# First batch of a 1-head attention layer: weighted sum by seven products instead of eight, and the next batch's norm reading its input from two separately fetched blocks

## The chip, the cores and the metric

The kernel runs on one core of a Trainium2 chip. The metric is device time in microseconds (us), median over runs. The engines that matter are TensorE (matrix products; "PE" in the profile), VectorE ("DVE"), ScalarE ("ACT"), GpSimd ("POOL") and SyncE ("SP"), on whose queue every DMA of the part concerned is issued. TensorE writes into PSUM[...].

## The reference

Input: 4 images ("batches") of 512 channels and 32x32 = 1024 tokens, float32. Four layers follow each other, each adding to its input. The change lies in the third, one attention head as wide as all channels:

```python
xf = jnp.transpose(x, (0, 2, 3, 1)).reshape(b, h * w, c)       # tokens x channels
mu = jnp.mean(xf, axis=-1, keepdims=True)
var = jnp.var(xf, axis=-1, keepdims=True)
xn = (xf - mu) * jax.lax.rsqrt(var + EPS) * norm_w
qkv = jnp.einsum('bnc,dc->bnd', xn, w_qkv) + b_qkv
q, k, v = jnp.split(qkv, 3, axis=-1)
attn = jax.nn.softmax(jnp.einsum('bqc,bkc->bqk', q, k) * c ** (-0.5), axis=-1)
out = jnp.einsum('bqk,bkc->bqc', attn, v)
out = jnp.einsum('bnc,dc->bnd', out, w_proj) + b_proj
return x + transpose(out)
```

The layer before it (a linear attention) ends with an update of x; the one after it is a 4-head attention with a group norm. The first is an 8-head attention.

## The kernel before

**Tiles.** Channels lie on the 128 partitions in NC = 4 chunks, tokens in NTB = 2 blocks of TB = 512. An x of one batch is a tile of 2 MB; two of them fit into the on-chip memory, the others wait in DRAM ("homes"): `away(b)` stores x of batch b, `back(b)` loads it again. Other tiles are reused by name: a new tile of a name waits until all readers of the one before are done. Names that matter: `rds` (1 MB), `many` (1 MB), both used by the first layer's attention; `row` (3 buffers of one 512-wide row, for the norm's sums); `pt` (4) and `sum` (2), for the softmax's exponentials; PSUM has four banks `acc` and two pairs of banks `sc`, from which the norm's `lnsums`, the row sums and layer 2's products take theirs.

**Seven products.** Nearly every matrix product is done in 2x2 blocks by a scheme of seven block products and 15 sums (`seven_products`, L711-824). The sums of the inputs run on VectorE (`sum_inputs`), those of the weights on GpSimd (`sum_weights`, L695-698), and each result is put together from the products by copies on ScalarE (L746) and additions out of PSUM on VectorE, the joins (L737 and its neighbours).

**The 1-head layer, per batch** (loop at L1754): (1) queries, by seven products (records at L707), with the key weights folded in, so that the scores are taken against the normed x itself; (2) the values (`project_v`, L832), with the output weights folded in; (3) the scores (`keys_first`, L839), 8 tiles of 128 keys x 1024 queries made in pairs of blocks, each finished tile going to ScalarE for its exponential (`exp`, L1237) and from there into a running sum on VectorE (L1240); (4) the weighted sum of the values, together with the sums over the partitions (`row_sums`, L1256, two-bank tile `rowsum`), their reciprocals (`invert`, L678), and `add_block`: times the reciprocal (L1263), plus bias, plus x (L1265). Steps 3 and 4 are `one_head` (L1217-1378).

In step 4 batch 0 differs from the others. For batch 0, `one_head` gets a list `parts`; each of the 8 output tiles (4 channel chunks x 2 token blocks) is accumulated in one PSUM bank by 8 products of 128x128 by 128x512 (L1277), and ahead of each output tile one entry of `parts` is run. For batches 1 to 3 the sum is by seven products with shapes of their own (L1316): 56 products in place of 64, with 16 sums of value tiles (128x256) and 16 sums of exponentials (128x512) on VectorE, and ten joins.

**The norm of the next batch** (`layer_norm`, L1550-1593) has four parts for each token block: add (three additions over the channel chunks, L1557 and L1559), center (a product with ones gives the column sums, L1565; x less the mean, four at L1567; squares on ScalarE L1572, summed by three additions L1576), spread (a product with ones gives the variance, L1581; square root on ScalarE L1583, reciprocal L1584) and scale (four at L1589). It reads x of its batch from the 2 MB x tile.

**Order of the work.** TensorE's instructions keep the order in which the code issues them (a manual schedule covers all of it). Other work is threaded in by hand: `pieces` is a list of small pieces, `slot()` runs one, and `seven_products` calls it at its last `slots` pairs of calls and after every second product of its main part; `flush()` runs what is left. The other engines' instructions are ordered by the framework's scheduler; `soon()` gives some of them a higher priority.

While batch 0 runs, the list `pieces` also holds layer 2's last work, on batch 3: `linear_attention(B - 1)`, whose last two pieces are the updates of x (L1520). One more piece then stores x of batch 3 and loads x of batch 1. That is where batch 1's x gets its tile: the two tiles hold batch 0 and batch 3 until then. For this reason batch 1's norm is in `parts` (so in step 4), while those of batches 2 and 3 are in `pieces` from before step 2 of the batch ahead.

Ahead of the layer lies the end of the first layer's last attention: `sum_shared` (L1011) turns row sums into reciprocals, writes them to a DRAM tile `quotients` (L1030) and reads them back spread over all partitions into `rds` (L1033), where `normalise` multiplies them in (L1051). After this come loads of the 1-head layer's weights on the same SyncE queue: into the `v` tiles (L546) and `wo`.

Of the kernel before, what the change touches and what calls it, by code (L numbers as in the profile page):

```python
# [13 lines left out]
F32 = mybir.dt.float32  # L14
# [4 lines left out]
P = 128  # L19
# [455 lines left out]
def plain_path(ctx: ExitStack, tc: tile.TileContext, d: dict, out: bass.AP, count):  # L475
# [23 lines left out]
    def acc_tile():  # L499
        return ps_acc.tile([P, TB], F32, tag="acc", name="acc")  # L500
# [7 lines left out]
    def pt_tile(name):  # L508
        return work.tile([P, 2, TB], F32, tag="pt", bufs=4, name=name)
# [4 lines left out]
    def many_tile(name):  # L514
        return work.tile([P, NC, TB], F32, tag="many", name=name)
# [9 lines left out]
    def chunks_tile(tag, name, bufs=1):  # L525
        return work.tile([P, NC, TB], F32, tag=tag, bufs=bufs, name=name)


    def load_wqkv(src):
        t = wpool.tile([P, NC, 3 * C], F32, tag="wqkv", name="wqkv")  # L530
        nc.sync.dma_start(t, src.rearrange("(c p) o -> p c o", p=P))
        return t

    def load_wo(src):
        t = wpool.tile([P, NC, C], F32, tag="wo", name="wo")
        nc.sync.dma_start(t, src.rearrange("(c p) o -> p c o", p=P))
        return t
# [33 lines left out]
    def away(b):  # L571
        homes[b] = dram.tile([P, NC, S], F32, tag=f"home{b}", bufs=1, name=f"home{b}")
        nc.sync.dma_start(homes[b], xs.pop(b))

    def back(b):
        nc.sync.dma_start(x_tile(b), homes.pop(b))
# [89 lines left out]
    def both(*fs):  # L666
        return lambda: [f() for f in fs]
# [8 lines left out]
    def invert(rd, ps):  # L676

        nc.vector.reciprocal(rd, ps)  # L678
        n, m = next(unit), rd.shape[0]
        for i, t in enumerate((ps, rd)):  # L680
            closing[:] = [nc.vector.tensor_reduce(tops[:m, i, n : n + 1], t, AX.X, ALU.max).ins]
# [532 lines left out]
        while parts:  # L1214
            parts.pop(0)()

    def one_head(b, q, ws, acc, xn, sums, v, scale, bias, room, between, parts):  # L1217

# [31 lines left out]
        def row_sums():  # L1253
            rows = two_tile("rowsum")
            for t in range(NTB):
                nc.tensor.matmul(  # L1256
                    rows[:, t, :], lhsT=ones, rhs=acc[:, t, :], start=True, stop=True
                )
            return rows

        def add_block(m, tb, t, source, quotient):

            nc.vector.tensor_tensor(t, source, quotient, ALU.mult)  # L1263
            xv = x[:, m, bass.ts(tb, TB)]
            nc.vector.scalar_tensor_tensor(xv, t, bias[:, m : m + 1], xv, ALU.add, ALU.add)  # L1265

        flush()
        between()

        if parts:  # L1270
            rds = chunks_tile("q0", "rd")
            for k, (qb, m) in enumerate(itertools.product(range(NTB), range(NC))):
                if parts:
                    parts.pop(0)()
                out = acc_tile()
                for i, j in enumerate(order):
                    nc.tensor.matmul(  # L1277
                        out, lhsT=v[j // 2][:, j % 2, bass.ts(m, P)], rhs=pts[j][:, qb, :],
                        start=(i == 0), stop=(i == NT - 1),
                    )  # L1280
                if k == 0:
                    rows = row_sums()
                if m == 0:
                    invert(rds[:, qb, :], rows[:, qb, :])
                add_block(m, qb, rds[:, NTB + k % 2, :], out, rds[:, qb, :])
            return

# [257 lines left out]
        ]  # L1547


    def layer_norm(b, tb, tiles):  # L1550

        x = lambda c: xs[b][:, c, bass.ts(tb, TB)]
        t = {}

        def add():
            s = t["s"] = row_tile("s")
            nc.vector.tensor_tensor(s, x(0), x(1), ALU.add)  # L1557
            for c in range(2, NC):
                nc.vector.tensor_tensor(s, s, x(c), ALU.add)  # L1559

        def center():
            xn = tiles[tb]
            t["ps"] = two_tile("lnsums")
            mean = t["ps"][:, 0, :]
            nc.tensor.matmul(mean, lhsT=ones, rhs=t["s"], start=True, stop=True)  # L1565
            for c in range(NC):
                nc.vector.scalar_tensor_tensor(  # L1567
                    xn[:, c, :], mean, -1.0 / C, x(c), ALU.mult, ALU.add
                )
            for c in range(NC):  # L1570
                sq = row_tile("sq")
                nc.scalar.activation(sq, xn[:, c, :], AF.Square)  # L1572
                if c == 0:
                    t["sq"] = sq
                else:
                    nc.vector.tensor_tensor(t["sq"], t["sq"], sq, ALU.add)  # L1576

        def spread():
            xn = tiles[tb]
            var = t["ps"][:, 1, :]  # L1580
            nc.tensor.matmul(var, lhsT=ones, rhs=t["sq"], start=True, stop=True)  # L1581
            rstd = t["rstd"] = row_tile("rstd")
            nc.scalar.activation(rstd, var, AF.Sqrt, bias=eps, scale=1.0 / C)  # L1583
            nc.vector.reciprocal(rstd, rstd)  # L1584

        def scale():
            xn, rstd = tiles[tb], t["rstd"]
            for c in range(NC):
                nc.vector.scalar_tensor_tensor(  # L1589
                    xn[:, c, :], xn[:, c, :], col("nw2", c), rstd, ALU.mult, ALU.mult  # L1590
                )

        return [add, center, spread, scale]
# [64 lines left out]
    with tc.manual_schedule(engines={mybir.EngineType.PE}):  # L1658
# [63 lines left out]
        loadedv = load_bias(d["bv2"], d["wo2n"], vt[2:], brows[:, 1, :])  # L1722
        flush()
        wo2 = load_wo(d["wo2"])
        lin = linear_attention(B - 1, lambda i: pt_tile("l1"))

        norms[1][0]()
# [26 lines left out]
        for b in range(B):  # L1754
            q = q_tiles()
            vt = v_tiles()
            after = normed_tiles(b + 1)

            def sums():
                if b == 0:  # L1760
                    made.extend(sum_inputs(spare, normed(xn)))
                return made

            half = NC // 2
            seven_products(
                half,
                lambda i, j, o: gq[:, 2 * j : 2 * j + 2, bass.ts(i * half + o, P)],
                normed(xn),
                lambda i, o: uq[:, i * half + o : i * half + o + 1],
                lambda i, tb, o: q[tb][:, i * half + o, :],  # L1770
                sums,
                slots=2,
            )

            pair = lambda t, i: t[:, 2 * i : 2 * i + 2, :]
            halves = work.tile([P, 2, 2, TB], F32, tag="os", name="qs")
            third = work.tile([P, 2, TB], F32, tag="oi", name="qs")
            places = [halves[:, 0], halves[:, 1], third, pair(q[1], 0)]
            sum_weights(places, lambda i, j: pair(q[i], j))
            if b == 0:  # L1780
                pieces.append(lambda: (away(B - 1), back(1)))
            parts = []
            if b + 1 < B:
                (add0, *n0), (add1, *n1) = [layer_norm(b + 1, tb, after) for tb in range(NTB)]
            if b == 0:

                parts = [
                    both(add0, n0[0]), idle, both(*n0[1:], add1), idle, n1[0], idle,
                    both(*n1[1:]), lambda: sum_inputs(spare, normed(after)),
                ]  # L1790
            elif b + 1 < B:
                pieces.extend([
                    add0, n0[0], idle, n0[1], n0[2], add1, n1[0], idle, n1[1], n1[2],
                ])
            else:
                first = chunks_tile("ot", "gn")
                loaded3 = load_bias(
                    d["bv3"], d["wo3n"], [after[1][:, 2 * i : 2 * i + 2, :] for i in range(2)]
                )
                loads3 = []  # L1800
                pieces.extend([
                    *group_norm(0, 0, first),
                    lambda: loads3.append(weighted_bias("bo3", loaded3)),
                ])
            project_v(vt, hv, normed(xn), made, wpool.tile([P, NC, C], F32, tag="wo", name="ws"))
            one_head(
                b, q, places, work.tile([P, 2, TB], F32, tag="ou", name="acc"), xn, made, vt,
                float(C) ** -0.5, bo2,
                after if b == B - 1 else [w2[:, NC : 2 * NC, :], w2[:, 2 * NC :, :]],
                lambda: b + 1 < B or loads3.insert(0, load_wqkv(d["wqkv3"])), parts,  # L1810
            )
            if 0 < b < B - 1:
                sum_inputs(spare, normed(after))
            away(b)
            back((b + 2) % B)
            if b + 1 < B:
                xn = after
# [103 lines left out]
```

## Time and profile before

| | |
|---|---|
| median of 3 runs | 2450.09 us (2449.71 to 2451.28) |
| the profiled execution | 2450.76 us, its span 2449.0 us |
| ScalarE busy, share of the span | 704.6 us, 29% |
| GpSimd busy, share of the span | 251.1 us, 10% |
| batch 0's scores, TensorE | 1043.28 to 1093.66 us |
| batch 0's weighted sum, with batch 1's norm | 1093.66 to 1153.74 us |
| batch 1's weighted sum | 1254.42 to 1304.35 us |

The shares are from the page's first part, the stages from the chain of waits. The chain is followed back from the last instruction of the run, at each step to what released it or to the instruction before it on its engine; a piece of it reads: start in us, length in us, engine, what it writes, line, and how many records. One product of 128x128 by 128x512 in float32 makes two records. A row of a group reads: line, engine, operation, out<-in with shapes, count; then busy time and the mean ns of one record; then the idle time just ahead of them on their engine, with what ended it. Records on TensorE are pipelined and overlap, so their mean ns is longer than the time from one to the next. In the timeline a line reads: start, length, engine, line and operation, and in brackets the idle time ahead with its releaser. In the busy time by stretches each engine has its busy us and number of instructions, then the granted clock of TensorE (PEclk, 1.00 is full), the DMA engines' busy share and GB/s.

### The profile page before, as it was taken

The page shows a single profiled execution, that of the slowest core. Times are in us where ns is not written, and L with a number is a line of the kernel's source. Part 1 is how long each engine was busy: PE and PEld are TensorE (multiplying, and loading weights), DVE is VectorE, ACT ScalarE, POOL GpSimd, SP SyncE. Part 2 cuts the span into 40 slices and gives each one's busy share as a digit, 9 for nine tenths or more (in the row PEclk, how much of TensorE's full clock was granted, in tenths as well). Part 3 has the DMA queues.
Part 4 walks back from the last instruction along what each step waited for, and adds up shares of the span by engine and source line. Part 5 has one row for each costly group of instructions (what it writes and reads, how often), then busy time and mean ns, then how long its engine had stood idle before and what let it go on. Part 6 is the DMA issues. An engine that isn't in the chain of part 4 may idle for free.

```text
span 2449.0 us, 24662 instructions
## 1 busy us (share of the span) xinstructions
PE 2433.3 (99%) x10098; PEld 1225.7 (50%) x10098; DVE 1506.1 (61%) x1798; ACT 704.6 (29%) x864; POOL 251.1 (10%) x240
## 2 busy tenths in 40 slices
PE   9999999999999999999999999999999999999999
PEld 4544544453455344644645446445556456555653
DVE  3677577757775788656595774763554554445344
ACT  1454144415531653221211201112321430332132
POOL 4001100110010001101103021021010001002000
PEclk9999999999999999999999999999999999999999
DMA  5000020002000301011001010110010001001001
GB/s 185 7 12 18 5 78 10 18 5 79 19 9 13 130 23 48 5 69 39 31 1 69 5 74 13 52 69 18 35 69 1 18 35 52 1 35 35 1 22 45
DMA packets 28959, 88.64 MB, mean 36 GB/s; under 512 B 2508, under 2 KB 10188, under 8 KB 25895
## 3 DMA queue, kind: packets, MB, share of 16 engines
q1 hardware_dynamic: 28838, 87.00, 9.9%
q8 instruction: 81, 1.33, 0.2%
q14 instruction: 40, 0.32, 0.0%
HBM read 60.59 MB, written 25.35 MB: 35 GB/s over the span
## 4 chain that ended last, share of the span: by engine, by line
PE 99%; DVE 1%; ACT 0%; issue 0%; DMA 0%; SPq 0%; DVEq 0%
PE acc L707 20%; PE acc L832 12%; PE acc L967 9%; PE acc L982 9%; PE sc L936 9%; PE sc L931 9%; PE acc L839 8%; PE acc L1084 7%; PE acc L1316 6%; PE acc L1277 2%; PE feat L641 1%; PE acc L1018 1%; PE acc L641 1%; PE upd L1520 1%; PE acc L1454 1%; PE xt L1425 1%
## 5 line engine op out<-in xcount | busy, mean ns | idle before, releaser
L941 ACT ACTIVATE pt<-sc 128x1024 f32<-128x1024 f32 x384 | 379.2, 1022 | 541.2 <-PE sc L936 304.0
L950 DVE TENSOR_TENSOR sum<-sum,pt 128x1024 f32<-128x1024 f32 x256 | 314.6, 1229 | 159.0 <-ACT pt L941 146.5
L967 PE MATMUL acc<-pt,v 64*64 64x512 f32 x2048 | 247.6, 591 | 0.0
L931 PE MATMUL sc<-q,k 64*64 64x512 f32 x2048 | 245.0, 591 | 1.1 <-ACT pt L941 1.1
L982 PE MATMUL acc<-pt,v 128*128 128x512 f32 x512 | 240.8, 594 | 0.0
L936 PE MATMUL sc<-q,k 128*128 128x512 f32 x512 | 239.9, 594 | 0.0
L707 PE MATMUL acc<-t,ws 128*128 128x512 f32 x384 | 173.9, 594 | 0.0
L695 POOL TENSOR_TENSOR ws<-wqkv 128x256 f32<-128x256 f32 (+1 forms) x40 | 39.7, 992 | 1307.1 <-PE acc L1018 523.2
L947 DVE TENSOR_TENSOR sum<-pt 128x1024 f32<-128x1024 f32 x64 | 78.0, 1219 | 137.4 <-ACT pt L941 137.4
L982 PEld LDWEIGHTS acc<-pt,v 128*128 128x128 f32 x512 | 96.8, 190 | 125.1 <-issue 121.4
L936 PEld LDWEIGHTS sc<-q,k 128*128 128x128 f32 x512 | 97.1, 191 | 115.9 <-issue 92.7
L967 PEld LDWEIGHTS acc<-pt,v 64*64 64x64 f32 x2048 | 78.3, 133 | 142.5 <-issue 140.3
L931 PEld LDWEIGHTS sc<-q,k 64*64 64x64 f32 x2048 | 77.3, 133 | 140.9 <-issue 131.9
L707 PEld LDWEIGHTS acc<-t,ws 128*128 128x128 f32 x384 | 72.6, 190 | 86.5 <-issue 85.0
L746 ACT COPY v<-acc 128x512 f32<-128x512 f32 x24 | 14.0, 585 | 308.6 <-PE acc L832 308.6
L678 DVE RECIPROCAL rd<-acc 128x512 f32<-128x512 f32 (+1 forms) x24 | 80.5, 3353 | 29.1 <-PE acc L1018 29.1
L832 PE MATMUL acc<-ws,t 128*128 128x256 f32 x384 | 87.3, 380 | 0.0
L839 PE MATMUL acc<-qs,w 128*128 128x512 f32 x192 | 86.6, 593 | 0.0
L839 PE MATMUL acc<-q,ln 128*128 128x512 f32 x192 | 85.8, 593 | 0.0
L1084 PE MATMUL acc<-ot,wo 128*128 128x256 f32 x336 | 80.7, 383 | 2.7 <-ACT ou L1103 2.7
L737 DVE TENSOR_TENSOR v<-acc,v 128x512 f32<-128x512 f32 x72 | 49.5, 689 | 51.5 <-PE acc L832 51.2
L746 ACT COPY q<-acc 128x512 f32<-128x512 f32 x40 | 23.4, 585 | 197.1 <-PE acc L707 197.1
(326 smaller groups left out, 3476.0 us busy)
## 6 DMA issues: line engine op xcount, KB each, us to landing
home<-x SPq DMA_DIRECT2D x8, 2048.0 KB
x<-home SPq DMA_DIRECT2D x8, 2048.0 KB
out<-x SPq DMA_DIRECT2D x32, 256.0 KB
rds<-quotients SPq DMA_DIRECT2D x30, 256.0 KB
rds<-quotients SPq DMA_DIRECT2D x7, 1024.0 KB
x<-in_x SPq DMA_DIRECT2D x3, 2048.0 KB
wo<-in_wo SPq DMA_DIRECT2D x3, 1024.0 KB
w<-in_w SPq DMA_DIRECT2D x1, 3072.0 KB
```

Of the source, the lines that this page charges most:

```text
L678: nc.vector.reciprocal(rd, ps)
L707: nc.tensor.matmul(ps, lhsT=w[:, m, :], rhs=x[:, m, :], start=start, stop=stop, skip_group_check=True)
L832: nc.tensor.matmul(ps[:, bass.ts(r, C // 2)], lhsT=x[:, m, bass.ts(2 * o + r, P)], rhs=w[:, m, :], start=(start and r == 0), stop=stop, sk ...
L839: nc.tensor.matmul(ps, lhsT=x[:, m, bass.ts(o, P)], rhs=w[:, m, :], start=start, stop=stop, skip_group_check=True,)
L931: nc.tensor.matmul(ps[half(h), s, :], lhsT=key(g, i)[half(s), half(h)], rhs=q[qb][half(s), g, :], start=True, stop=True,)
L936: nc.tensor.matmul(ps[:, s, :], lhsT=key(g, 2 * i + s), rhs=q[qb][:, g, :], start=True, stop=True)
L941: exps.append(nc.scalar.activation(pt, ps, AF.Exp, scale=scale).ins)
L950: adds.append(nc.vector.tensor_tensor(acc, acc, pt, ALU.add).ins)
L967: nc.tensor.matmul(outs[qb, g][r][half(s), :], lhsT=v[i // 2][half(r), i % 2, g * P + s * hd : g * P + (s + 1) * hd], rhs=pt[half(r), s, : ...
L982: nc.tensor.matmul(outs[qb, g][0], lhsT=v[j // 2][:, j % 2, bass.ts(g, P)], rhs=pt[:, s, :], start=(j == 0), stop=(j == NT - 1),)
L1084: nc.tensor.matmul(ps[i][:, bass.ts(o, n)], lhsT=w[:, m, bass.ts(o, P)], rhs=t[:, m, :], start=(start and m + o == 0), stop=(stop and m == ...
L1316: nc.tensor.matmul(ps[i, o], lhsT=w[m][:, bass.ts(o, P)], rhs=t[m], start=(start and m == 0), stop=(stop and m == 3), skip_group_check=True,)
```

## The change

`one_head` loses the argument `parts` and the branch for batch 0, so all four batches take their weighted sum by seven products. The pieces of batch 1's norm now go into `pieces` ahead of step 2, as they do for the later batches. At that time x of batch 1 has no x tile yet, so `layer_norm` gets an argument `copies`: two 1 MB tiles, one for each token block, fetched from the same DRAM home. Block 0 is fetched into a tile of name `rds` before layer 2's pieces are put on the list; block 1 into a tile of name `many`, in the piece that also stores batch 3 and loads batch 1. The full x of batch 1 is still loaded as before, for the result's addition. Batch 1's sums of inputs, which were the last entry of `parts`, are now issued after `one_head`, as for batches 1 and 2.

```diff
-    def one_head(b, q, ws, acc, xn, sums, v, scale, bias, room, between, parts):
+    def one_head(b, q, ws, acc, xn, sums, v, scale, bias, room, between):
...
         flush()
         between()
-
-        if parts:
-            rds = chunks_tile("q0", "rd")
-            for k, (qb, m) in enumerate(itertools.product(range(NTB), range(NC))):
-                if parts:
-                    parts.pop(0)()
-                out = acc_tile()
-                for i, j in enumerate(order):
-                    nc.tensor.matmul(
-                        out, lhsT=v[j // 2][:, j % 2, bass.ts(m, P)], rhs=pts[j][:, qb, :],
-                        start=(i == 0), stop=(i == NT - 1),
-                    )
-                if k == 0:
-                    rows = row_sums()
-                if m == 0:
-                    invert(rds[:, qb, :], rows[:, qb, :])
-                add_block(m, qb, rds[:, NTB + k % 2, :], out, rds[:, qb, :])
-            return
...
-    def layer_norm(b, tb, tiles):
+    def layer_norm(b, tb, tiles, copies=None):
-        x = lambda c: xs[b][:, c, bass.ts(tb, TB)]
+        x = lambda c: copies[tb][:, c, :] if copies else xs[b][:, c, bass.ts(tb, TB)]
...
         wo2 = load_wo(d["wo2"])
+
+        copies = []
+
+        def copy_next(t):
+            nc.sync.dma_start(t, homes[1][:, :, bass.ts(len(copies), TB)])
+            copies.append(t)
+
+        copy_next(work.tile([P, NC, TB], F32, tag="rds", name="x1"))
         lin = linear_attention(B - 1, lambda i: pt_tile("l1"))
...
             if b == 0:
-                pieces.append(lambda: (away(B - 1), back(1)))
-            parts = []
+                pieces.append(lambda: (copy_next(many_tile("x1")), away(B - 1), back(1)))
             if b + 1 < B:
-                (add0, *n0), (add1, *n1) = [layer_norm(b + 1, tb, after) for tb in range(NTB)]
-            if b == 0:
-
-                parts = [
-                    both(add0, n0[0]), idle, both(*n0[1:], add1), idle, n1[0], idle,
-                    both(*n1[1:]), lambda: sum_inputs(spare, normed(after)),
+                (add0, *n0), (add1, *n1) = [
+                    layer_norm(b + 1, tb, after, None if b else copies) for tb in range(NTB)
                 ]
-            elif b + 1 < B:
                 pieces.extend([
                     add0, n0[0], idle, n0[1], n0[2], add1, n1[0], idle, n1[1], n1[2],
                 ])
...
-            if 0 < b < B - 1:
+            if b < B - 1:
                 sum_inputs(spare, normed(after))
```

More of the change, by code (lines that the diff above doesn't have):

```diff
@@ L1809, in plain_path @@
                 after if b == B - 1 else [w2[:, NC : 2 * NC, :], w2[:, 2 * NC :, :]],
-                lambda: b + 1 < B or loads3.insert(0, load_wqkv(d["wqkv3"])), parts,
+                lambda: b + 1 < B or loads3.insert(0, load_wqkv(d["wqkv3"])),
             )
-            if 0 < b < B - 1:
+            if b < B - 1:
                 sum_inputs(spare, normed(after))
```

## The prediction

> **What bounds the kernel now.** I read, in this order: busy time and the chain that ended last on the page, the groups by line and form around the change, the busy time of each engine in four stretches, VectorE's timeline of the next batch, and SyncE's timeline.
>
> ```profile
> PE 2433.3 (99%) x10098; PEld 1225.7 (50%) x10098; DVE 1506.1 (61%) x1798; ACT 704.6 (29%) x864; POOL 251.1 (10%) x240
> ...
> PE 99%; DVE 1%; ACT 0%; issue 0%; DMA 0%; SPq 0%; DVEq 0%
> ```
>
> TensorE is busy throughout and the chain runs along it: a product removed is time removed, unless a wait comes in.
>
> ```profile
> L1277 PE MATMUL acc<-pt,v 128*128 128x512 f32 x96 | 42.5, 593 | 0.0
> ...
> L1277 PE MATMUL acc<-pts,v 128*128 128x512 f32 x32 | 15.0, 593 | 0.0
> ```
>
> Batch 0's weighted sum is 128 records. The 593 ns overlap: the chain gives
>
> ```profile
> 1125.41 13.73 PE acc L1277 x32
> ...
> 1269.87 34.47 PE acc L1316 x80
> ```
>
> so a record takes 13.73/32 = 0.429 us of TensorE, a 128x512 product (two records) 0.858. Batch 1 computes the same sum by seven products, at the same pace (34.47/80 = 0.431).
>
> ```profile
> core 0: us, PE busy (x) PEld busy (x) DVE busy (x) ACT busy (x) POOL busy (x), PEclk, DMA share, GB/s
> 1062.00:1093.40 31.40, 31.40 (x76) 13.82 (x73) 21.28 (x29) 8.25 (x8) 0.00 (x0) 1.00 0.34 134
> 1093.40:1153.60 60.20, 60.20 (x142) 26.68 (x141) 48.20 (x54) 9.16 (x13) 2.35 (x2) 1.00 0.00 0
> 1204.40:1254.30 49.90, 49.90 (x117) 22.21 (x118) 34.23 (x50) 15.70 (x21) 0.00 (x0) 1.00 0.00 0
> 1254.30:1304.20 49.90, 49.90 (x118) 21.98 (x117) 41.39 (x56) 2.63 (x4) 5.13 (x5) 1.00 0.00 0
> ```
>
> Rows one and two are batch 0's scores (from where layer 1's last update leaves them) and weighted sum; three and four are batch 1's. Read the VectorE column: 21.28+48.20 = 69.5 of 91.6 us in batch 0. VectorE has slack here, but not much.
>
> ```profile
> 1269.91 3.36 DVE L678 RECIPROCAL ln<-rowsum 128x512 f32<-128x512 f32 x1 [3.37 <-PE rowsum L1256]
> ...
> 1274.92 3.35 DVE L678 RECIPROCAL ln<-rowsum 128x512 f32<-128x512 f32 x1
> ...
> 1279.31 0.68 DVE L1263 TENSOR_TENSOR ln<-acc,ln 128x512 f32<-128x512 f32 x1
> ```
>
> In batch 1 VectorE is ahead: it waits 3.37 us for the row sums. Its L1263 then frees a PSUM tile that TensorE's product at 1280.05 takes at once: no margin there if VectorE comes late.
>
> **What the Trainium skill says.** "Perfetto Trace Analysis", Identifying the Most-Contended Engine: matmul busy share does not tell how near the roofline a kernel is. The trace agrees: 99% says nothing of the spare product that seven products save. "VectorE: DVE Perf Modes", The TRN2 errata: an fp32 tensor_tensor of 512 columns takes 691 ns; the rows here have 680 to 693, and successive starts lie 0.60 apart. "TensorE: Matmul & The Clock Gate", HAM oscillation: idle gaps of TensorE over about 3.4 us can halve its clock; before has no such gap after its start (PEclk 1.00), so no run shows it. "DMA: Bandwidth & Descriptors", Bandwidth: 1 MB in 6.15 us; the trace's 2 MB store takes 6.4 us from issue to the next one, which gives 3.2 for 1 MB.
>
> **The change, part by part.**
>
> Removed: 64 products become 56. 8 x 0.858 = 6.87 us of TensorE. The four norm products (3.43) and two row sums (1.72) stay.
>
> Added on VectorE: seven products need 16 sums of 128x256 (spacing 0.34: 5.5 us), 16 of 128x512 (0.60: 9.6) and 10 joins (about 0.65: 6.5), 21.6 in all. Batch 0's scores and sum then hold 69.5+21.6 = 91.1 us of VectorE, less 1.8 for the first block's sums, which the built order has before 1062; TensorE's time shrinks to 91.6-6.87 = 84.7. VectorE becomes the bound. By total alone: 89.3 of work, and about 7 us before 1073 in which it still waits for the first score products (6.1 us of idle ahead of batch 0's L737 now), make 96: 5 us more than 91.6.
>
> Moved: both norms of batch 1 go from the weighted sum into batch 0's scores. Layer 1's pieces hold the slots up to 1062, so first norm, second norm and the score joins crowd into 31 us. By the built order TensorE's queue has: centre product (block 0) before the last joins of the first score half, spread product 8 products later, centre product (block 1) 12 later, spread product 4 later, then the weighted sum. TensorE runs in order, so each waits with everything behind it. I laid VectorE's instructions out in the built order, each as soon as VectorE is free and what it waits for is done, with durations from before (0.60 a 512 operation, 1.13 a 1024, 3.29 a reciprocal, 0.68 a scale, 0.34 a 256):
>
> 1. Centre product at 1072.8. VectorE first finishes an exp sum (to 1074.8), then 4 centres, 3 square sums, 4 score joins, another exp sum: 11x0.60+1.13 = 7.7, +0.2 latency: 1082.7. TensorE arrives at 1072.8+9x0.858 = 1080.5. Wait 2.3.
> 2. From 1082.6: exp sum 1.13, two adds of block 1's sum 1.2, two small sums 0.7, a join 0.6, reciprocal 3.3, five joins 3.0, four scales 2.7, exp sum 1.1, last add 0.7: 14.4, 1097.0, +0.3 for products not ready. TensorE arrives at 1082.8+13x0.858 = 1094.0. Wait 3.4.
> 3. Centre result at 1098.4; 4 centres, 2 joins, 3 square sums, an exp sum: 9x0.60+1.13 = 6.5, 1105.1. TensorE arrives at 1097.3+5x0.858 = 1101.6. Wait 3.5.
> 4. From 1105.0: exp sum 1.1, the norm's reciprocal and scales 6.0, and the weighted sum's sums (14x0.34, 13x0.60: 12.6) end at 1124.5. TensorE needs the first of them at 1105.1+17x0.858+1.72 = 1121.4 (made at 1118, no wait). But the row sums' first reciprocal starts at 1124.5, not at 1121.6: the join behind it ends 1129.1 where TensorE wants its PSUM tile at 1128.3 (wait 0.9), and L1263, after the second reciprocal, ends 1134.6 against 1132.6 (wait 2.1).
>
> Sum of waits 2.3+3.4+3.5+0.9+2.1 = 12.2; with spacings rounded up 12.7; I take 12.4. The same laying-out on before gives batch 1's product at 1280.0 (trace 1280.05) and no wait in batch 0 (trace: none). ScalarE's exps and squares are ready before VectorE asks; an extra table load (1.28) lies in its idle time.
>
> Fetches: two 1 MB loads on SyncE's queue.
>
> ```profile
> 904.10 0.53 SPq L1030 DMA_DIRECT2D quotients<-rd  x1
> ...
> 905.86 1.24 SPq L1033 DMA_DIRECT2D rds<-quotients  x2
> ...
> 916.06 3.82 SPq L546 DMA_DIRECT2D v<-in_wqkv  x2
> ```
>
> In the built order block 1's load stands ahead of the first of these. It waits for the product that reads `many`, done at 900.7, so it transfers 3.2 us (6.15 by the page) from about 901 and may hold the quotients back 0 to 2.5 us. Behind them waits VectorE's L1051 at 910.95; but VectorE idles 3.89 us at 933.31, before TensorE's next need: 0 (at most 1 if that cover fails). Block 0's load waits for L1051's reads and goes out near 912, ahead of the v loads at 916.06: 0. Both blocks land by 920 and are read after 1030. The store of batch 3 and load of batch 1 stay, now needed only at the end of batch 1.
>
> What follows: batch 1's sums of inputs (four 1.22) go after the sum as in the later batches, which show no wait for them; the store of batch 0 and load of batch 2 keep their distance to batch 1's start (18 us until first read). 0.
>
> Total -6.87+12.4 = +5.5 on the profiled execution, 2450.76 (span 2449.0 and 1.8 around it): 2456.3. The median shown is 0.67 below that run: 2450.09+5.5 = 2455.6.
>
> **Rivals.**
>
> A, hidden: VectorE keeps up and the whole 6.87 is gained, 2443.2. For: batches 1 and 2 do these products without waits. Against: their first norm lies in the v projection, where VectorE has room; here both norms share the scores. This needs 12.4 us less VectorE work on TensorE's path.
>
> B, half: the waits at the norm products hold, but VectorE catches up in the weighted sum (or spacings are tighter): the last two waits, 3.0, go: 2452.6, within the noise.
>
> C, more: waits of 3.4 and 3.5 us let TensorE's clock fall for a window each (half of 3.4 us lost, an estimate from the clock gate page), or the fetch delays the quotients: +1.7 to +3.4, 2457.3 to 2459.0. For: the gaps are as long as the window. Against: it must fall on a gap exactly.
>
> That the change doesn't do what it says: the built order has 56 products there, so no.
>
> **How the numbers follow.** VectorE-bound as laid out 0.64, A 0.06, B 0.15, C 0.15. A measurement of this kernel tells 0.2% (4.9 us) from no change: the line lies at 2455.0. The first case spreads over 2454.5 to 2457 and is beyond the line nine times in ten (0.58), with C 0.73 slower; its rest and B, 0.21 same; A, 0.06 faster. Range 2452.6 (B) to 2459.0 (C); it leaves out A and little else.
>
> **What would show it.** After: 112 records of weighted sum in batch 0; TensorE idle about 2, 3.5 and 3.5 us ahead of the three later norm products, released by VectorE's square sum, add and square sum; about 3 us in the weighted sum; VectorE busy without a break from 1073 to 1140; the rowsum reciprocal with no idle before it; L1051 at 911 nearly unmoved. Wrong if TensorE's chain has no such waits (A), if PEclk dips or L1051 waits some us longer (C), or if VectorE idles before the rowsum reciprocal (B).

## The result, and the profile after

The changed kernel takes 2457.3 us (median of 8 runs, 2456.22 to 2460.36) beside 2450.02 us before (8 runs, 2449.71 to 2451.28): ratio 1.0029, 95% interval 1.0020 to 1.0038. It is 7.3 us slower. The eight products are gone, and the time is not.

The profiled execution took 2460.36 us (span 2458.6), which is the longest of the eight, so its own surplus (9.6 us) is larger than the median's. The page's first part and its chain:

```profile
PE 2430.8 (99%) x10082; PEld 1218.5 (50%) x10082; DVE 1527.9 (62%) x1840; ACT 708.5 (29%) x868; POOL 253.3 (10%) x240
...
PE 96%; DVE 2%; issue 1%; DMA 0%; ACT 0%; SPq 0%; DVEq 0%
```

TensorE has 16 records fewer, VectorE 42 instructions and 21.8 us more. The chain, which lay on TensorE at 99%, now crosses over to VectorE for 2%. Where it does so is seen in TensorE's timeline; these are all of its waits from the scores to the end of the weighted sum (in brackets: idle time and releaser):

```profile
1083.14 1.78 PE L1565 MATMUL lnsums<-sq,ones 128*128 128x512 f32 x2 [2.08 <-DVE sq L1560]
1099.44 1.13 PE L1549 MATMUL lnsums<-s,ones 128*128 128x512 f32 x2 [3.18 <-DVE s L1543]
1108.82 1.13 PE L1565 MATMUL lnsums<-sq,ones 128*128 128x512 f32 x2 [3.12 <-DVE sq L1560]
1132.58 3.70 PE L1297 MATMUL acc<-w 128*128 128x512 f32 x8 [0.32 <-DVE ln L1307]
1138.17 3.70 PE L1297 MATMUL acc<-ts,ln 128*128 128x512 f32 x8 [1.89 <-DVE ln L1262]
```

Five waits, 10.59 us, all released by VectorE: first block's spread product, second block's centre and spread products, and two products of the weighted sum that need a PSUM tile. (These lines have numbers 16 to 19 smaller than in the kernel before: L1565 is the spread product, L1549 the centre, L1297 the weighted sum.) The busy time by stretches shows what VectorE had to do, and something else:

```profile
1062.00:1162.50 100.50, 89.91 (x201) 38.29 (x200) 88.42 (x121) 20.86 (x24) 6.26 (x6) 0.97 0.11 42
1083.48:1086.89 3.41, 3.41 (x5) 1.33 (x4) 2.62 (x5) 1.92 (x2) 0.00 (x0) 0.50 0.00 0
1100.55:1103.96 3.41, 3.41 (x6) 1.35 (x5) 1.93 (x4) 1.86 (x3) 0.00 (x0) 0.50 0.00 0
```

In the first row VectorE (third pair) is busy 88.42 us; before, it was 69.5 in the same work. In the other two the granted clock of TensorE (last number but two) is 0.50, for 3.41 us right behind the first wait and again right behind the second, where before had 1.00 throughout. Half of 3.41, 1.7 us, is lost in each of these two dips.

The balance of this execution, from the start of batch 0's scores (1043.56; before 1043.28) to the next batch's queries (1162.47; before 1153.74): 118.91 us for 110.46, so 8.45 longer. -6.87 for the products, +10.59 of waits, +3.4 for the two dips, and the remaining 1.3 for five restarts, about 0.27 each: without a wait the next record starts some 0.17 us before the one ahead of it has ended, and the two records behind a wait are followed by the next 0.96 us after their start (1108.82 to 1109.78) in place of 0.86. Outside the stage the two executions differ by 1.14: 0.28 ahead of it and 0.86 at the very end, behind the last product. The 0.28 is itself the sum of two things: the stretch with the fetch is 1.27 longer (see below), and up to there this execution was 0.99 ahead, 0.98 of it from the first 56 us, long before anything that the change touches.

### The profile page after: what moved, and what is told of

It reads as the page before. It is cut to its first block, busy times and chain, and to the rows that moved or that the text cites. A ratio compares the mean times of both kernels' runs of the same rounds, so it can differ in the third digit from the quotient of the medians.

```text
span 2458.6 us, 24682 instructions
## 1 busy us (share of the span) xinstructions
PE 2430.8 (99%) x10082; PEld 1218.5 (50%) x10082; DVE 1527.9 (62%) x1840; ACT 708.5 (29%) x868; POOL 253.3 (10%) x240
## 3 DMA queue, kind: packets, MB, share of 16 engines
q8 instruction: 81, 1.33, 0.2%
## 4 chain that ended last, share of the span: by engine, by line
PE 96%; DVE 2%; issue 1%; DMA 0%; ACT 0%; SPq 0%; DVEq 0%
PE acc L707 20%; PE acc L832 11%; PE acc L982 9%; PE sc L936 9%; PE acc L967 9%; PE sc L931 9%; PE acc L839 8%; PE acc L1084 7%; PE acc L1297 7%; PE feat L641 1%; PE acc L1018 1%; PE acc L641 1%; PE upd L1501 1%; PE acc L1435 1%; PE xt L1406 1%; PE kv L641 1%
```

## The experiments

Each was timed in five rounds beside the kernel before, on one chip for each group of four. "Laid out" in the expectations is the working of the prediction, repeated on the changed build: VectorE's instructions in their order, each as soon as VectorE and its inputs are ready.

**1. Filling the waits.** The question is whether the waits themselves or their effect on the clock account for all that exceeds the prediction's sum.

```diff
+        def fill(ps, n):
+            for _ in range(n):
+                nc.tensor.matmul(ps, lhsT=ones, rhs=bv1, start=True, stop=True)
...
+            if copies and tb:
+                fill(t["ps"][:, 1, :], 3)
             nc.tensor.matmul(mean, lhsT=ones, rhs=t["s"], start=True, stop=True)
...
+            if copies:
+                fill(var, 3 if tb else 2)
             nc.tensor.matmul(var, lhsT=ones, rhs=t["sq"], start=True, stop=True)
```

> The changed kernel with idle TensorE time before the three late norm products filled: 2, 3 and 3 spare products of 128x512 (0.86 us each) on constant data into the norm's own free PSUM half, ahead of the first spread, the second centre and the second spread product. Theory 1 (VectorE-bound waits of 2 to 3.5 us, and on top a lower TensorE clock after such gaps): fillers disappear in the waits, the granted clock stays at 1.00 from 1062 to 1142, and the time is 2450.0 + 3.2 (the laid-out waits less 6.87, the build shifting a few of VectorE's instructions in the weighted sum by 2.1 us in our favour) + about 1.3 for the fetch = 2453 to 2455. Theory 2 (the clock dips are chance and cost nothing in the median; what exceeds my sum is something else): 2457.3 - 2.1 = 2455.2 or more, with dips as before. If the waits are not waits for VectorE at all, the fillers add 8 x 0.86 = 6.9: 2464.

Measured: 2453.96 us against 2450.8, ratio 1.0014 (1.0008 to 1.0021): 3.2 us over before, where the changed kernel is 7.3 over, although TensorE does 6.9 us of work that nobody needs. TensorE's timeline and the busy time by stretches:

```profile
1081.61 1.12 PE L1573 MATMUL lnsums<-sq,ones 128*128 128x512 f32 x2 [0.36 <-DVE sq L1566]
1096.22 1.12 PE L1555 MATMUL lnsums<-s,ones 128*128 128x512 f32 x2 [0.60 <-DVE s L1547]
1104.05 1.13 PE L1573 MATMUL lnsums<-sq,ones 128*128 128x512 f32 x2 [0.69 <-DVE sq L1566]
...
```

```profile
1081.60:1085.00 3.40, 3.39 (x8) 1.63 (x9) 3.40 (x6) 1.97 (x2) 0.00 (x0) 1.00 0.00 0
...
1096.20:1099.60 3.40, 3.38 (x8) 1.63 (x9) 3.32 (x5) 1.45 (x3) 0.00 (x0) 1.00 0.00 0
1099.60:1103.00 3.40, 3.40 (x9) 1.25 (x7) 3.40 (x6) 3.25 (x5) 0.00 (x0) 1.00 0.00 0
```

The fillers vanish in the waits, which still end on the same VectorE operations, and the clock stays at 1.00 (last column but two). Of the 4.1 us between this kernel's surplus (3.2) and the changed kernel's (7.3), 1.8 are a shift of the build in its favour: fillers and waits together are 8.8 us in its trace (6.87+1.97), where the changed kernel waits 10.6. Some 2.3 remain for the clock and for what differs outside the stage, an estimate from one trace of each. That the dips come with the idle time and go with it is in the records.

**2. The norm moved, the plain products kept.**

```diff
+        if b == 0:
+            rds = chunks_tile("q0", "rd")
+            for k, (qb, m) in enumerate(itertools.product(range(NTB), range(NC))):
...
```

The loop is that of the kernel before, without `parts`.

> The changed kernel, but batch 0's weighted sum again by 64 plain products without the seven products' sums on VectorE; only the norm has moved and its x is fetched. Theory 1 (the crowd of norms and joins in the scores makes the waits): waits of 2.3 and 7.5 us before the two spread products, none in the weighted sum, no product saved: 2450.0 + 9.8 + 1.3 for the fetch + 1.7 to 3.4 for the clock = 2461 to 2465. Rival (the norm is free where it is now, the extra sums of the seven products are the cost): 2450 to 2452.

Measured: 2462.39 us, ratio 1.0048 (1.0034 to 1.0062): 11.6 us slower than before, as theory 1 has it. TensorE's timeline has two waits and no other:

```profile
1081.66 1.13 PE L1581 MATMUL lnsums<-sq,ones 128*128 128x512 f32 x2 [2.08 <-DVE sq L1576]
1106.33 2.07 PE L1581 MATMUL lnsums<-sq,ones 128*128 128x512 f32 x2 [7.26 <-DVE sq L1576]
```

So the norm is not free in its new place, whatever becomes of the weighted sum. Both norms, with a reciprocal of 3.3 us ahead of the last score joins, stand in VectorE's queue between these joins. VectorE's total load is not what makes the waits here:

```profile
1062.00:1166.00 104.00, 94.66 (x212) 41.20 (x212) 66.47 (x79) 19.39 (x22) 2.50 (x4) 0.95 0.10 41
```

It is busy 66.47 of 104.00 us, and TensorE still waits 9.34. Each against its own before, the changed kernel is 4.3 us faster than this one: given the norm's new place, the seven products gain. The counterpart, seven products with the norm left in the weighted sum, was not run.

**3. The additions on GpSimd.**

```diff
-            nc.vector.tensor_tensor(s, x(0), x(1), ALU.add)
+            eng = nc.gpsimd if copies else nc.vector
+            eng.tensor_tensor(s, x(0), x(1), ALU.add)
             for c in range(2, NC):
-                nc.vector.tensor_tensor(s, s, x(c), ALU.add)
+                eng.tensor_tensor(s, s, x(c), ALU.add)
```

> The changed kernel with batch 1's norm additions (six of 128x512) on GpSimd. Theory 1 (VectorE's total work sets the end, the place of a wait doesn't matter): the wait of the second centre product goes, but the wait of the second spread product grows from 3.5 to about 7.3 us; in all 11.2 of waits for 12.2: 1 us less than the changed kernel, 2455 to 2458. Rival (each wait has its own price): the 3.2 us of that wait and its clock dip of 1.7 go: 2452.5.

Measured: 2459.67 us, ratio 1.0036 (1.0022 to 1.0050), 8.9 over before and above the range that theory 1 gave. TensorE's waits:

```profile
1082.00 1.12 PE L1566 MATMUL lnsums<-sq,ones 128*128 128x512 f32 x2 [2.08 <-DVE sq L1561]
1092.70 2.71 PE L839 MATMUL acc<-q,ln 128*128 128x512 f32 x4 [2.71 <-DVE pt L737]
1109.47 2.07 PE L1566 MATMUL lnsums<-sq,ones 128*128 128x512 f32 x2 [7.08 <-DVE sq L1561]
```

The centre's wait is gone and the spread's is 7.08 (7.3 expected), and the time is 7 us above the rival's; but a wait of 2.71 at a score product is new, so this is not the clean test of the rival that it was meant to be (experiment 5 is). GpSimd's and VectorE's timelines show where the new wait comes from:

```profile
1082.08 2.13 POOL L1542 TENSOR_TENSOR s<-x 128x512 f32<-128x512 f32 x1 [53.03 <-DVE sq L1561]
1084.29 2.73 POOL L1544 TENSOR_TENSOR s<-s,x 128x512 f32<-128x512 f32 x2
```

```profile
1083.00 2.90 DVE L1291 TENSOR_TENSOR ln<-v,v 128x256 f32<-128x256 f32 x2
1085.82 1.82 DVE L1291 TENSOR_TENSOR w<-ln,v 128x256 f32<-128x256 f32 x2
...
1109.34 0.75 DVE L1291 TENSOR_TENSOR ln<-v,v 128x256 f32<-128x256 f32 x2
```

The same pair of VectorE sums takes 2.90 us while GpSimd adds and 0.75 us when it doesn't; the four together take some 3 us more than they do later, and the join that the score product waits for stands behind them in VectorE's queue. The Trainium skill's page "SBUF — State Buffer", section "SBUF: two separate sides", says that VectorE, with two on-chip inputs, and GpSimd share a port pair that whoever starts first holds for its whole instruction. The trace agrees.

**4. The running sum of exponentials on GpSimd.**

```diff
-                nc.vector.tensor_tensor(acc, acc if len(taken) > 2 else taken[0], pt, ALU.add)
+                eng = nc.vector if b else nc.gpsimd
+                eng.tensor_tensor(acc, acc if len(taken) > 2 else taken[0], pt, ALU.add)
```

> The changed kernel with batch 0's running sum of exponentials (seven additions of 128x1024, 7.9 us of VectorE) on GpSimd. If only VectorE's count of work decides: waits shrink to 1.8, 2.7 and 0.3 us, 4.8 in all for 6.87 saved: 2450.8 - 2.1, with small restarts 2449 to 2450. Theory P, from the run with the adds on GpSimd, where VectorE's 128x256 sums of two on-chip operands took about 1.4 us each for 0.34 while GpSimd worked: GpSimd's 7 x 2.3 = 16 us slow VectorE by several us, and nothing is won against the changed kernel: 2456 to 2462.

Measured: 2466.82 us, ratio 1.0065 (1.0051 to 1.0079): 15.9 us over before, the slowest of all and above theory P's range. Waits of 3.59, 5.48, 6.26 and 0.17 us; each of the first three is followed by a clock below 1.00. VectorE's timeline, beside GpSimd's additions of 2.4 us:

```profile
1077.69 2.49 DVE L1561 TENSOR_TENSOR sq<-sq 128x512 f32<-128x512 f32 x1
1080.10 2.55 DVE L1292 TENSOR_TENSOR ln<-v,v 128x256 f32<-128x256 f32 x1
...
1083.77 0.41 DVE L1292 TENSOR_TENSOR ln<-v,v 128x256 f32<-128x256 f32 x1
```

Two GpSimd additions run here from 1077.26 to 1082.37, and the two VectorE operations beside them end at 1080.18 and 1082.65. Taking 7.9 us of work off VectorE made it later: GpSimd did not lighten its load.

**5. The spread product later.** Its piece and the scales go from ahead of the weighted sum to behind its first 16 products, in batch 0.

```diff
         p2(0)
         p2(1)
+        for f in late:
+            f()
         rows = row_sums()
...
+                late = [] if b else n1[1:]
                 pieces.extend([
-                    add0, n0[0], idle, n0[1], n0[2], add1, n1[0], idle, n1[1], n1[2],
+                    add0, n0[0], idle, n0[1], n0[2], add1, n1[0], *([idle, *n1[1:]] if b else []),
                 ])
```

> The changed kernel with the second spread product and its scales issued after the first 16 products of the weighted sum, in place of right ahead of it. Theory 1: its wait of 3.1 us goes, but VectorE is as late as before and TensorE waits in the weighted sum, 1.2 and 4.6 us by laying out: 11.4 in all for 12.2, 2455.5 to 2458. Rival (the wait stems from too few products between centre and spread): the wait is gone for good, 2454, or 2452.5 with one clock dip fewer.

Measured: 2459.13 us, ratio 1.0035 (1.0022 to 1.0049), 8.3 over before: no faster than the changed kernel. TensorE's waits:

```profile
1083.00 1.12 PE L1567 MATMUL lnsums<-sq,ones 128*128 128x512 f32 x2 [2.08 <-DVE sq L1562]
1097.61 1.12 PE L1551 MATMUL lnsums<-s,ones 128*128 128x512 f32 x2 [3.18 <-DVE s L1545]
1129.81 3.70 PE L1297 MATMUL acc<-ts,ln 128*128 128x512 f32 x8 [1.04 <-DVE ln L1307]
1137.92 6.50 PE L1297 MATMUL acc<-ts,v 128*128 128x512 f32 x8 [4.41 <-DVE ln L1307]
```

The wait of 3.12 is gone, and 1.04+4.41 have come in the weighted sum for 0.32+1.89: 10.71 in all, where the changed kernel has 10.59. The time is 1 us above theory 1's range and 5 above the rival's. VectorE is as late as before; only the place where TensorE meets this has moved. In this execution the first two waits, equal to those of the changed kernel, left the clock at 1.00, and the wait of 4.41 took it to 0.50. That gives the price of one dip directly: the second centre product starts 14.61 us behind the first spread product here and 16.30 in the changed kernel, 1.69 later.

**6. and 7. VectorE's work and its order, apart.** If VectorE's load is the cause, work that ScalarE can do must go there. The four reciprocals cost VectorE 13.2 us; as the exponential of a negative logarithm (exp(-ln), in the norm exp(-ln/2) in place of square root and reciprocal) they are two ScalarE operations each, and ScalarE is busy 20.86 us of 100.50 in this stage.

```diff
             rstd = t["rstd"] = row_tile("rstd")
+            if copies:
+                nc.scalar.activation(rstd, var, AF.Ln, bias=eps, scale=1.0 / C)
+                nc.scalar.activation(rstd, rstd, AF.Exp, scale=-0.5)
+                return
...
-        nc.vector.reciprocal(rd, ps)
+        if by_scalar:
+            nc.scalar.activation(rd, ps, AF.Ln)
+            nc.scalar.activation(rd, rd, AF.Exp, scale=-1.0)
+        else:
+            nc.vector.reciprocal(rd, ps)
```

> The changed kernel with the four reciprocals of 128x512 in batch 0 (two of batch 1's norm, two of the row sums; 13.2 us of VectorE) made by ScalarE as exp of minus the logarithm; order of the products as in the changed kernel. Laid out: the two waits of the weighted sum go, the first spread's 2.3 stays, the second centre's goes, the second spread's becomes 6.7: 9.0 for 6.87 saved, +2.1, and with clock dips of 1.7 to 3.4: 2454 to 2457. Rival (VectorE's total alone decides, the order is indifferent): the waits sink to near zero: 2444 to 2446.

Measured: 2454.29 us, ratio 1.0015 (1.0009 to 1.0022), 3.4 over before and in the first range. The waits of the weighted sum are gone, and at the norm's products two are left:

```profile
1082.03 1.13 PE L1569 MATMUL lnsums<-sq,ones 128*128 128x512 f32 x2 [2.08 <-DVE sq L1564]
1104.38 2.07 PE L1569 MATMUL lnsums<-sq,ones 128*128 128x512 f32 x2 [6.63 <-DVE sq L1564]
```

The order alone, with the reciprocals where they were: experiment 5's late spread, and the pieces of batch 0 spaced (the edit is shown against experiment 5).

```diff
-                    add0, n0[0], idle, n0[1], n0[2], add1, n1[0], *([idle, *n1[1:]] if b else []),
+                    both(add0, add1) if not b else add0, n0[0], idle, *([] if b else [idle]),
+                    n0[1], n0[2], *([add1] if b else []), n1[0], *([idle, *n1[1:]] if b else []),
```

> The changed kernel with the spaced norm pieces alone, reciprocals on VectorE. Laid out: the waits at the norm's products all but go (0.6), and one wait of about 13 us comes in the weighted sum, ahead of a product that needs a PSUM tile freed after the row sums' reciprocals: 13.8 for 6.87 saved, +6.9, with 1.7 to 3.4 for the clock 2459 to 2461. Rival (the order of the norm's products is the whole fault): 2444 to 2446.

Measured: 2458.61 us, ratio 1.0034 (1.0022 to 1.0046), 7.7 over before. The norm's waits are down to one, and a single long one has come in the weighted sum:

```profile
1083.12 1.12 PE L1567 MATMUL lnsums<-sq,ones 128*128 128x512 f32 x2 [0.38 <-DVE sq L1562]
1130.61 2.07 PE L1297 MATMUL acc<-pts,w 128*128 128x512 f32 x2 [12.89 <-DVE pts L1291]
```

The time is 0.4 under the range for the laid-out case, and far from the rival's. The wait's length is as laid out (13.2). Its releaser is not a PSUM tile behind the reciprocals, as the expectation named it, but a sum of exponentials (L1291) that VectorE reaches only behind the three reciprocals from 1112.11 on.

**8. Both together.**

> The same reciprocals on ScalarE, and the norm's pieces spaced: both blocks' additions first, the first spread product 12 products behind its centre in place of 8, the second spread product after 16 products of the weighted sum. Laid out: waits of 0.6 us in all: 2450.8 - 6.3 = 2444.5, up to 2446 with restarts and no clock dip. If the cost of the change lies elsewhere than in VectorE's work and its order (in the fetch, say), the time stays above 2450.

Measured: 2443.42 us (2442.86 to 2444.64), ratio 0.9969 (0.9957 to 0.9982): 7.5 us faster than before, where the changed kernel is 7.3 slower. TensorE's only wait in the stage, and the stage by stretches:

```profile
1085.66 1.13 PE L1571 MATMUL lnsums<-sq,ones 128*128 128x512 f32 x2 [0.38 <-DVE sq L1566]
```

```profile
1062.00:1093.40 31.40, 31.02 (x76) 13.33 (x73) 25.04 (x39) 12.94 (x14) 0.00 (x0) 1.00 0.34 134
1093.40:1148.60 55.20, 55.20 (x130) 24.42 (x129) 49.58 (x77) 17.80 (x21) 4.85 (x6) 1.00 0.00 1
```

TensorE is busy 86.22 of 86.60 us, the clock is full, and VectorE's 74.62 us (for 88.42) now leave it room. Measured like the balance above, the stage takes 104.25 us for 110.46 before: -6.21, the 6.87 of eight products less one wait and its restart. The fetch and the seven products of the change are all in this kernel: with room on VectorE, the products gain what they were to gain, and the fetch costs 1.03 us in this trace (see below), so neither explains the changed kernel's loss. Load and order were each tried with and without the other: at the same order, taking the reciprocals off VectorE is worth 3.9 us (changed kernel to experiment 6) or 15.2 (7 to 8); at the same load the other order is worth nothing (changed kernel to 7) or 10.9 (6 to 8, both with 74.6 us of VectorE's work).

The changed kernel and the eight beside one another: waits laid out and measured, the stage's length less that of before (110.46), and the median less that of before in the same comparison, all in us. The fillers' row has what is left of the waits beside the fillers.

| kernel | waits laid out | waits in the trace | stage | median |
|---|---|---|---|---|
| the changed kernel | 12.2 | 10.6 | +8.5 | +7.3 |
| fillers | 3.2 | 2.0 | +3.7 | +3.2 |
| norm moved, plain products | 9.8 | 9.3 | +13.4 | +11.6 |
| additions on GpSimd | 11.2 | 11.9 | +10.0 | +8.9 |
| exponentials' sum on GpSimd | 4.8 | 15.5 | +16.8 | +15.9 |
| late spread | 11.4 | 10.7 | +7.7 | +8.3 |
| reciprocals on ScalarE | 9.0 | 8.7 | +4.0 | +3.4 |
| order alone | 13.8 | 13.3 | +8.5 | +7.7 |
| reciprocals and order | 0.6 | 0.4 | -6.2 | -7.5 |

## Why the prediction was right, and where its sum was off

**The direction and the mechanism were right.** The products went as counted, TensorE came to wait for VectorE, and the five waits stand where the prediction put them, with the releasers it named. VectorE's work was expected at 89.3 us and is 88.42. The first step came out to the tenth: TensorE was to start the spread product at 1082.8, and did at 1083.14, of which 0.28 is the later start of the stage. The laying-out is the argument that the runs bear out. The reckoning "by total alone", which gave nearly the same figure, would have found no wait in experiment 2, where VectorE is busy 66.47 of 104.00 us; that it agreed is luck. Of the 10.59 us, 8.38 lie in the scores, where the norms and the joins meet, and 2.21 in the weighted sum, with the sums of the seven products.

**Terms of the sum were mis-sized, with opposite signs.** The prediction counts a wait from where the next product would have started, the trace from the end of the last record, some 0.17 us later. In the prediction's terms the waits are 2.25, 3.35, 3.29, 0.49 and 2.06, for 2.3, 3.4, 3.5, 0.9 and 2.1: 11.4 us for the 12.4 that it took. Against this, what follows a wait was left out of the main case: 0.10 us behind each, 0.5 in all, and the clock, 3.4 in the profiled execution. There the forecast was +5.5 and the result +9.6: -1.0 for the waits, +0.5, +3.4, +1.3 for the fetch, -1.0 at the start of the run and +0.9 at its end.

**Rival C had the clock, with the wrong waits.** It named dips of 1.7 us behind the waits of 3.4 and 3.5 us, with a chance of 0.15 together with a held-up fetch; they came behind the first (2.08) and the second (3.18), and not behind the third (3.12). By the prediction's own sign for C, "if PEclk dips", this part of C came true beside the main case. The median, 2457.3, lies at the lower end of C's 2457.3 to 2459, 0.3 above the range of the main case and 1.7 over its forecast. "It must fall on a gap exactly" was the argument against C. Place does decide, as the last section shows, but 2.08 us of idle time in the right place were enough. Of the eight executions the mean clock is on record: 0.998 for two, the profiled one and the fastest, and 0.999 for six. One dip takes 0.0007 off it, and the kernel before, without a dip, reads 0.999 or 1.000; so most of the unprofiled executions had probably one dip, not two (an estimate).

**The dips also moved the later steps.** The second centre product was to start at 1097.3 and came at 1099.44, since the 26 records ahead of it, held up by the first dip, made VectorE's joins wait for TensorE; VectorE was therefore not busy without a break from 1073 to 1140, as "what would show it" had it, but idle for 1.62 us ahead of 1087.72 and for 1.42 ahead of 1103.91; experiment 5, which has no dip there, shows only 0.16 in the scores.

**The fetch was costed at nothing, with the wrong cover.** The prediction hid a late L1051 behind VectorE's idle time at 933. In this trace the reload of the quotients ended later (before, then after), and the wait came sooner, at a product of layer 1's last attention:

```profile
910.95 1.30 DVE L1051 TENSOR_TENSOR ot<-ot,rds 128x512 f32<-128x512 f32 x2 [0.63 <-DMA rds<-quotients]
911.23 1.29 DVE L1051 TENSOR_TENSOR ot<-ot,rds 128x512 f32<-128x512 f32 x2 [1.90 <-DMA rds<-quotients]
914.31 0.65 PE L999 MATMUL acc<-sum,ones 64*64 64x512 f32 x3 [0.73 <-DVE ot L978]
```

The idle time of 0.73 us understates it. From the row-sum product L1018 to the first product of L641 TensorE took 25.72 us before (898.77 to 924.49) and 26.99 here (897.78 to 924.77): 1.27 more. It is 1.03 more in the kernel of experiment 8 and 0 to 0.24 in the other seven. So L1051 at 911 only looks "nearly unmoved": the execution was 0.99 us ahead until then. The price can exceed the "at most 1" that was kept for it. Why the reload ends later in two of nine executions is open: in those compared (the changed kernel, experiments 1, 6 and 8) the fetch goes out at the same distance, 1.13 us, from the product L1018.

**Rivals A and B.** A (2443.2, all hidden) asked for 12.4 us less of VectorE's work on TensorE's path. Experiments 6 and 8 bear on this: 13.2 us less alone gives 2454.29, and with the products spaced as well 2443.42. B, VectorE catching up in the weighted sum, didn't happen: 2.2 us of waits stayed there.

What stays open: how the 1.7 us between forecast and median divide between dips, restarts and fetch, of which the unprofiled runs keep only the rounded clock.

## What to carry to other kernels

A trade of TensorE products for VectorE sums must be priced in the stage where both run, by laying out VectorE's queue. A share of 61% over the whole span said nothing of these 90 us, and the stage's total says too little as well: a kernel with VectorE busy 66.5 of 104 us made TensorE wait 9.3 us (experiment 2), and two with the same 74.6 us of VectorE's work lie 10.9 us apart by the order of the norm's pieces (experiments 6 and 8). While VectorE stays late, moving a wait to another place gives nothing back (experiments 5 and 7); what helps is work taken off that engine and, with it, more products between a request and its use, and each without the other fell short here. Look for an engine that doesn't hold up the one to be relieved: here ScalarE took the work with no new wait for TensorE, and GpSimd made VectorE slower.

## What the runs showed of the hardware that was not expected

TensorE's clock fell behind every idle gap of 3.59 us or more in this stage of the traces (8 of 8, up to 12.89 us), to half for 3.4 us or more, and behind 4 of the 9 gaps of 2.08 to 3.18 us; the same gap of 2.08 us at the same product did it in two executions and not in three. The Trainium skill's page "TensorE: Matmul & The Clock Gate", section "HAM oscillation — how this bites in real kernels", has it for gaps above about 3.4 us; the traces agree for these, but shorter gaps did it as well, and what decided was where they lay. In each trace the clock changes only at points that are multiples of 3.413 us apart; in the changed kernel at 1083.48, 1086.89, 1100.55 and 1103.96. Four stretches of that grid hold most of the three waits for the norm:

```profile
1080.07:1083.48 3.41, 1.33 (x4) 0.46 (x3) 3.41 (x6) 1.43 (x2) 0.00 (x0) 1.00 0.00 0
...
1097.14:1100.55 3.41, 1.11 (x3) 0.63 (x4) 3.38 (x4) 0.00 (x0) 0.00 (x0) 1.00 0.02 5
...
1103.96:1107.37 3.41, 1.74 (x4) 0.43 (x3) 3.41 (x6) 2.59 (x3) 0.00 (x0) 1.00 0.00 0
1107.37:1110.79 3.42, 1.97 (x5) 1.02 (x6) 3.42 (x6) 2.12 (x3) 0.00 (x0) 1.00 0.00 0
```

In the first two TensorE (first pair) is busy 1.33 and 1.11 us, so idle 2.08 and 2.30, and the stretch behind each of them has the clock of 0.50 shown above. The third wait, 3.12 us, lies across two stretches, 1.67 and 1.45 idle, and the clock stays full. The ten traces cut in this way, 310 stretches between 1058 and 1168, fall apart cleanly: at full clock, each of the 12 stretches with 2.08 us or more idle was followed by half clock, and none of those with 1.84 or less; at half clock, each of 9 with 1.15 us or more idle was followed by another at half, and each of 12 with 0.23 or less by full clock. In these traces, then, a gap of up to 1.84 us never cost clock, and whether one of 2 to 3 us did was a matter of chance, of where it fell on the grid. The idle time is as the profile gives it, and it models the ends of products.

And GpSimd additions lengthen VectorE's sums of two on-chip operands from 0.41 to 2.55 us (experiment 4), about GpSimd's own 2.4 us for one instruction: in that trace VectorE's operation ends 0.28 us behind GpSimd's. Beside the same additions, VectorE's operations with one operand in PSUM kept their time (L1552 there, three in 1.89 us at 1073.49; in the changed kernel three such, L1551 at 1100.61, take the same 1.89).
